# Layer 1's dilated convolution as row differences: four products for two output rows in place of six

## The chip, the cores and the metric

One Trainium2 chip, one core of it. The metric is the device time in microseconds (us) of one execution of the kernel.

## The reference

Two layers run one after the other on an input of 32 images, 128 channels, 56 x 56 pixels, all in fp32. Layer 0 is a depthwise 7 x 7 convolution, a layer norm, and a mixture of eight experts with two experts for each token and a capacity for each expert; its result is added to the input and to the normed convolution. Layer 1 takes that as `x`:

```python
feat = conv2d(x, conv_w, padding=DIL, dilation=DIL)      # 3x3, DIL = 3, 128 -> 64 channels
feat = batchnorm(feat, bn1_g, bn1_b, bn1_m, bn1_v)
feat = jax.nn.gelu(feat, approximate=False)
F2 = jnp.fft.fft2(feat.astype(jnp.float32), axes=(-2, -1))
...
out_f = jnp.abs(jnp.fft.ifft2(out_f, axes=(-2, -1)))     # attention over 8 channels of a head
...
gate = jnp.abs(jnp.fft.ifft2(gate, axes=(-2, -1)))       # F2 times a sigmoid gate
y = jnp.concatenate([out_f, gate], axis=1)
return y + x
```

The change concerns the first line: output row h is the sum over three kernel rows of products with the input rows h - 3, h and h + 3.

## The kernel before

**Layer 0.** The depthwise convolution and the norm write tokens to `xf` in HBM. The search for each expert's capacity and the lists of its tokens follow, and the experts run one after the other: tokens are gathered from `xf` (line 1048), multiplied by `W1` (line 1071, `ph`) and `W2` (line 1089, `py`), and stored to `yf` by slot. Expert 7 is the last.

**The gathers of layer 1.** A token of layer 1 is the sum of its row of `xf` and two rows of `yf`. A *row* here is a block of 8 image rows of two images, 7 x 128 tokens. `release` (line 458) issues one indirect DMA on GpSimd's queue (POOL) that gathers 128 tokens into a slice of a tile `y`; fourteen make a row, seven rows make a pair of images, and 16 pairs make 1568 gathers. `total` adds the two `y` tiles of a row to `xa` (line 474, two tensor_tensor on VectorE, each of 128 x 896) and stores the sum to `xsum`. `bring` makes sure of the sum and loads the row from `xsum` again; `place` turns it (line 1290) and adds it with beta to the padded input `xp` in SBUF (line 1294).

Each gather waits for the matmul that was the newest when the gather sixteen places ahead of it was asked for (`gated`, with `leash["n"]` of 16), and for one of six `y` tiles, which are three rows. How far apart gathers are asked for in the program is `PACE`, in units of matmul columns, of which MAIN counts those of `back` and FRONT those of `front`. `total` of a row comes in the program two rows ahead of its `place` at the latest, so VectorE, which works its queue in order, meets the wait for the last gather of a row at that point. The first gathers are issued while expert 7 still runs.

**Layer 1's two halves.** `front(pr)` makes the input of a pair of images and convolves it: for each block of 8 rows nine taps, each tap a matmul of 448 columns for either image (line 1305), the two images in the two halves of the array's columns (64 output channels each) and of the bank `pf`, then one Gelu with scale and shift on ScalarE (line 1313). `back(pr)` does the transforms as turns and products (lines 1348 and 1356), the Gram product `pg` (line 1380), the attention (lines 1445 and 1446), the gate (line 1494) and the outputs `oa` and `ob` (lines 1461 and 1524). VectorE copies each turned bank to `mid` (line 1335), ScalarE copies the products out (line 1359).

**The order.** It is written out by generators: while `back(pr)` runs, `front(pr + 1)` is fed in after the first sixth of MAIN, in proportion to the columns done. `front(0)` runs alone ahead of the loop and `back(15)` alone at its end. Each yield of `front` is the grain in which it is fed: 448 columns for a `place`, 1344 for three taps.

Pools that the change touches: `d4` (four `xp` tiles), `d6` (six `xa` and six `y`), `ring` (six `mid`, and six `o` that hold `oa` and `ob`), `psum_f` (two banks `pf`).

Of the kernel before, what the change touches and what calls it, by code (L numbers as in the profile page):

```python
# [38 lines left out]
C = 128  # L39
H = W = 56  # L40
RP = 59
# [33 lines left out]
def conv_seq_kernel(ctx: ExitStack, tc: tile.TileContext, t: dict, out: bass.AP, dbg: dict):  # L75
# [366 lines left out]
    def release():  # L442
# [6 lines left out]
        if k == 0:  # L449
            xs = d6.tile([128, NB, C], F32, name="xa", tag="xa")  # L450
            nc.sync.dma_start(out=xs, in_=xfv[:, r * NB : (r + 1) * NB, :])
            begun_[r] = xs, []
# [46 lines left out]
    def inputs(pr):  # L499
        xps = [d4.tile([C, XL], F32, name="xp") for i in range(2)]  # L500
        for i in range(2):
            nc.sync.dma_start(out=xps[i], in_=t["xp"][pr + i * HI])
        return xps
# [21 lines left out]
    if True:  # L525
# [638 lines left out]
        for e in range(E):  # L1164
# [6 lines left out]
            if e == E - 1:  # L1171
# [5 lines left out]
                d4 = ctx.enter_context(tc.tile_pool(name="d4", bufs=4))  # L1177
                d6 = ctx.enter_context(tc.tile_pool(name="d6", bufs=6))
# [62 lines left out]
    d2 = ctx.enter_context(tc.tile_pool(name="d2", bufs=2))  # L1241
    ring = ctx.enter_context(tc.tile_pool(name="ring", bufs=6))
    psum = ctx.enter_context(tc.tile_pool(name="psum_d", bufs=5, space=PSUM))
# [21 lines left out]
    bsc, bsh = batchnorm("bn1")  # L1265

# [16 lines left out]
    def place(r, xps):  # L1283
        xs, rb = rows.pop(r), r % NB
        for m0 in range(0, NB, 4):
# [5 lines left out]
            for i in range(2):  # L1291
                px = interior(xps[i], rb * P8, P8)[:, :, m0 * P8 : (m0 + nm) * P8]
# [4 lines left out]

    def front(pr, xps, feat):


        def taps(pf, g, k0):
            for k in range(k0, k0 + 3):
                o = ((k // 3) * 3 + 8 * g) * RP + (k % 3) * 3
                for i in range(2):
                    step["pe"] = nc.tensor.matmul(  # L1305
                        pf[i * DD : (i + 1) * DD, : 8 * W],
                        lhsT=cw[:, k, :],
                        rhs=xps[i][:, o : o + 8 * RP].rearrange("p (h w) -> p h w", w=RP)[:, :, :W],
                        start=(k == 0),
                        stop=(k == 8),  # L1310
                    )
            if k0 == 6:
                nc.scalar.activation(  # L1313
                    feat[:, 8 * g * W : 8 * (g + 1) * W], pf[:, : 8 * W], AF.Gelu, scale=bsc, bias=bsh
                )

# [5 lines left out]
        for g in range(NB):  # L1322
            if g + 1 < NB:
                place(pr * NB + g + 1, xps)
                bring(pr * NB + g + 3)
                yield NB * 64
            pf = psumf.tile([128, 512], F32, name="pf")
# [369 lines left out]
```

## Time and profile before

| | |
|---|---|
| median of three runs | 5202.68 us (5199.97 to 5206.07) |
| the profiled execution's own time | 4783.52 us |
| its span, first to last instruction | 4781.7 us |
| mean granted TensorE clock | 0.972 |
| busy: PE, DVE, ACT, POOL | 4479.7, 2812.1, 2087.5, 2627.5 us |
| first gather of layer 1's rows begins, last one ends | 2583.2 us, 4656.0 us |
| first matmul of layer 1's convolution | about 2795 us |

PE is TensorE, PEld its weight loads, DVE VectorE, ACT ScalarE, POOL GpSimd. An fp32 matmul or weight load stands in the trace as two records, one for each pass, so the 2016 matmuls of the convolution are 4032 records. Matmuls of the two images run beside each other. A group row names the line, the engine, the tiles written and read, the shape and the count; behind the first bar stand the busy time in us and the mean duration of one in ns, behind the second the idle time ahead of the group. In the timeline and the chain the first number is the start and the second the length, in us.

### The profile page before, as it was taken

What the parts mean: (1) busy time and instruction counts of PE and PEld (TensorE: products, weight loads), DVE (VectorE), ACT (ScalarE), POOL (GpSimd) and SP (SyncE); (2) the same over time, 40 slices, a digit from 0 to 9 for tenths busy, and PEclk for the clock granted to TensorE, in tenths of its full rate; (3) what the DMA queues carried; (4) which work ended last, traced back from release to release, by engine and by line L of the source; (5) the groups of instructions that cost most, each with busy time, mean ns of one, the idle gap of its engine ahead of it and who ended that gap; (6) DMA issues with size and microseconds to landing.
All of it is one profiled execution on the core that took longest, in us unless ns stands there. A gap on an engine that the chain in (4) does not pass through costs nothing.

```text
span 4781.7 us, 87262 instructions
## 1 busy us (share of the span) xinstructions
PE 4479.7 (94%) x33034; PEld 3134.7 (66%) x33034; DVE 2812.1 (59%) x5863; ACT 2087.5 (44%) x4260; POOL 2627.5 (55%) x2633
## 2 busy tenths in 40 slices
PE   7888872899999999999999989999999999999999
PEld 6777762577777777777777755666565555555556
DVE  4778787786857685735212325555555555555556
ACT  2657672344444444444444423333333333333334
POOL 0000010455555666666663777777677777777770
PEclk9999985899999999999999999999999999999999
DMA  9989953122222233333336766666666766666652
GB/s 251 268 253 268 271 157 99 49 63 65 67 69 70 77 84 84 87 87 89 86 89 191 187 150 179 181 182 183 177 174 183 184 185 175 178 184 178 184 154 59
DMA packets 767736, 705.23 MB, mean 147 GB/s; under 512 B 73231, under 2 KB 679568, under 8 KB 763220
## 3 DMA queue, kind: packets, MB, share of 16 engines
q1 hardware_dynamic: 597060, 487.55, 34.3%
q0 software_dynamic: 81664, 167.15, 16.2%
q10 hardware_dynamic: 88592, 44.96, 3.3%
q8 instruction: 261, 4.28, 0.4%
q14 instruction: 159, 1.30, 0.1%
HBM read 472.99 MB, written 226.39 MB: 146 GB/s over the span
## 4 chain that ended last, share of the span: by engine, by line
PE 75%; DVE 3%; DMA 3%; issue 2%; POOL 1%; ACT 0%; DVEq 0%; SPq 0%; POOLq 0%; ACTq 0%
PE py L1089 18%; PE ph L1071 17%; PE pf L1305 16%; PE pm L1356 8%; PE pt L1348 4%; PE pxt L1054 2%; PE pg L1380 2%; DMA y<-yf,slot 2%; PE pre L1445 2%; PE pxs L1290 2%; PE pim L1446 2%; DVE junk L716 1%; POOL y L458 1%; PE pid L956 1%; PE pn L745 1%
## 5 line engine op out<-in xcount | busy, mean ns | idle before, releaser
L458 POOL DMA_INDIRECT y<-yf,slot x1568 | 1567.0, 999 | 559.7 <-issue 318.6
L1048 POOL DMA_INDIRECT xg<-xf,ids x861 | 914.0, 1062 | 670.9 <-PE py L1089 294.2
L1089 PEld LDWEIGHTS py<-W,hT 128*128 128x128 f32 x7872 | 918.7, 191 | 101.2 <-issue 58.4
L1089 PE MATMUL py<-W,hT 128*128 128x128 f32 x7872 | 932.5, 276 | 0.0
L1071 PE MATMUL ph<-xT,W 128*128 128x512 f32 (+1 forms) x1984 | 895.3, 590 | 0.0
L1305 PE MATMUL pf<-xp,cw 128*64 128x448 f32 x4032 | 886.7, 549 | 0.1
L1074 ACT ACTIVATE hT<-ph,b1t 128x512 f32<-128x512 f32 (+1 forms) x992 | 620.5, 671 | 58.5 <-PE ph L1071 44.3
L1123 ACT ACTIVATE yo<-yo,gates 128x128 f32<-128x128 f32 x861 | 275.2, 390 | 840.2 <-DVE yo L1103 840.2
L1103 DVE TENSOR_TENSOR yo<-py,b2t 128x512 f32<-128x512 f32 (+2 forms) x256 | 170.5, 669 | 716.0 <-issue 527.3
L1071 PEld LDWEIGHTS ph<-xT,W 128*128 128x128 f32 x1984 | 354.9, 191 | 327.8 <-issue 317.0
L1305 PEld LDWEIGHTS pf<-xp,cw 128*64 128x64 f32 x4032 | 276.4, 135 | 410.7 <-issue 373.9
L1335 DVE COPY mid<-pt 112x512 f32<-112x512 f32 (+3 forms) x480 | 308.3, 661 | 292.1 <-PE pt L1348 287.9
L220 POOL TENSOR_SCALAR y<-y,sd,nb 128x128 f32<-128x128 f32 x49 | 24.6, 517 | 694.3 <-PE plq L277 693.1
L474 DVE TENSOR_TENSOR xa<-xa,y 128x896 f32<-128x896 f32 x224 | 243.7, 1088 | 111.4 <-DMA y<-yf,slot 101.2
L225 ACT ACTIVATE y<-y,nb,sd 128x128 f32<-128x128 f32 x735 | 287.7, 482 | 31.6 <-DVE nb L212 31.6
L1359 ACT COPY T<-pm 128x464 f32<-128x464 f32 (+2 forms) x240 | 124.2, 519 | 379.9 <-PE pm L1356 379.8
L174 PE MATMUL psa<-xt,stay 112*64 112x98 f32 (+1 forms) x4608 | 229.1, 258 | 42.7 <-DVE y L182 23.2
L174 PEld LDWEIGHTS psa<-xt,stay 112*64 112x64 f32 (+1 forms) x4608 | 214.7, 144 | 53.3 <-DVE y L182 31.1
L182 DVE TENSOR_TENSOR y<-psa,dwbB 128x392 f32<-128x392 f32 x256 | 140.4, 557 | 174.6 <-PE psa L174 131.5
L1294 DVE SCALAR_TENSOR_TENSOR xp<-pxs,beta,xp 128x256 f32<-128x256 f32 x448 | 172.3, 444 | 91.9 <-PE pxs L1290 82.0
L1313 ACT ACTIVATE feat<-pf,bn_shift,bn_scale 128x448 f32<-128x448 f32 x112 | 81.0, 724 | 306.9 <-PE pf L1305 306.4
L716 DVE TENSOR_SCALAR_CACHE_REDUCE junk<-key,trial 112x896 f32<-112x896 f32 x168 | 188.7, 1145 | 4.2
(412 smaller groups left out, 6028.7 us busy)
## 6 DMA issues: line engine op xcount, KB each, us to landing
xt<-in_x_dram SPq DMA_DIRECT2D x256, 392.0 KB
yf<-yo SPq DMA_DIRECT2D x240, 256.0 KB
xp<-in_xp_dram SPq DMA_DIRECT2D x32, 1832.0 KB
xa<-xf SPq DMA_DIRECT2D x112, 448.0 KB
xsum<-xa SPq DMA_DIRECT2D x112, 448.0 KB
xs<-xsum SPq DMA_DIRECT2D x112, 448.0 KB
xf<-y ACTq DMA_DIRECT2D x42, 1024.0 KB
y<-yf,slot POOLq DMA_INDIRECT x1568
```

Of the source, the lines that this page charges most:

```text
L174: nc.tensor.matmul(ps[h * 64 : (h + 1) * 64, c * TG : (c + 1) * TG], lhsT=wts[b][:, c4 + c, :], rhs=xv[: PKS[b], c, h, :, b * NB : b * NB ...
L225: nc.scalar.activation(yi, yi, AF.Identity, scale=sd[:, i : i + 1], bias=nb[:, i : i + 1])
L458: gated(marks[max(0, n - leash["n"])], nc.gpsimd.indirect_dma_start(out=begun_[r][1][-1][:, m, :], out_offset=None, in_=yf[: 1 + reach(r), :],
L474: nc.vector.tensor_tensor(out=xs, in0=xs, in1=y, op=ALU.add)
L1048: paced(2 * q, nc.gpsimd.indirect_dma_start(out=xg[:n, q, :], out_offset=None, in_=xf, in_offset=bass.IndirectOffsetOnAxis(ap=ids[:n, c0 + ...
L1071: step["pe"] = nc.tensor.matmul(ph[:, :ns], lhsT=W1[:, e, f * C : (f + 1) * C], rhs=xT[:, :ns], start=True, stop=True)
L1074: gelu = nc.scalar.activation(hT[:, f, :ns], ph[:, :ns], AF.Gelu, bias=b1t[:, e, f : f + 1])
L1089: step["pe"] = nc.tensor.matmul(py[:n, q * C : (q + 1) * C], lhsT=hT[:, f, q * 128 : q * 128 + n], rhs=W2[:, e, f, :], start=(f == 0), sto ...
L1123: nc.scalar.activation(yo[:n, q], yo[:n, q], AF.Copy, scale=gates[:n, c0 + q : c0 + q + 1])
L1305: step["pe"] = nc.tensor.matmul(pf[i * DD : (i + 1) * DD, : 8 * W], lhsT=cw[:, k, :], rhs=xps[i][:, o : o + 8 * RP].rearrange("p (h w) -> ...
L1335: step["dve"] = nc.vector.tensor_copy(to, of)
L1356: step["pe"] = nc.tensor.matmul(pm[:, i * M : (i + 1) * M], lhsT=mid[:m, i, :], rhs=by, start=True, stop=True)
```

## The change

For input rows d0, d3, d6 and d9 that lie three apart, and the three kernel rows g0, g1 and g2, the output rows h and h + 3 are

    m0 = (d0 - d6) g0        m1 = (d6 + d3) (g0 + g1 + g2)/2
    m2 = (d6 - d3) (g0 - g1 + g2)/2      m3 = (d9 - d3) g2
    row h = m0 + m1 + m2,    row h + 3 = m1 - m2 + m3

with three column taps in each product. A group is six output rows (three times two); there are nine full groups and one of two rows, which takes three products.

- Once, ahead of layer 1: four small VectorE operations make the mixed weights.
- `lift`: for each group four tensor_tensor on VectorE, SBUF to SBUF, both images at once, 128 x 2 x 180 elements (121 in the last group, three of them), into `tt` (five buffers), one group ahead of its products.
- `taps`: 24 matmuls of 168 columns for a full group (18 of 112 for the last) into two banks `pf`, `mid_` (m1, m2) and `side` (m0, m3).
- Out of PSUM: ScalarE copies `mid_` to `feat`; VectorE adds m1 to `side` in place, then makes the two row sets from `side` and `feat`; Gelu runs on `feat` in place.
- In two of the four transforms of `back` the copies to `mid` of every other bank go from VectorE to ScalarE (`shared=True`).
- The two images' `xp` become one tile (`dx`, two buffers); `xa` has four buffers in place of six; `oa` and `ob` get a pool of their own with five buffers; FRONT, and so PACE, follow the smaller count of columns. The order of the gathers on POOL's queue is as before.

```diff
@@ release
-            xs = d6.tile([128, NB, C], F32, name="xa", tag="xa")
+            xs = d4.tile([128, NB, C], F32, name="xa", tag="xa")
@@ inputs
-        xps = [d4.tile([C, XL], F32, name="xp") for i in range(2)]
+        xp = dx.tile([C, 2, XL], F32, name="xp")
...
@@ weights
+    mixed = d1.tile([C, 2, 3, DD], F32, name="mixed")
+    cu = [cw[:, 0:3, :], mixed[:, 0], mixed[:, 1], cw[:, 6:9, :]]
+    nc.vector.tensor_tensor(out=cu[2], in0=cu[0], in1=cu[3], op=ALU.add)
+    nc.vector.tensor_tensor(out=cu[1], in0=cu[2], in1=cw[:, 3:6, :], op=ALU.add)
+    nc.vector.tensor_tensor(out=cu[2], in0=cu[2], in1=cw[:, 3:6, :], op=ALU.subtract)
+    nc.vector.tensor_scalar(out=mixed, in0=mixed, scalar1=0.5, scalar2=None, op0=ALU.mult)
@@ front
+    SEED = {0: (0, 6, ALU.subtract), 1: (6, 3, ALU.add), 2: (6, 3, ALU.subtract), 3: (9, 3, ALU.subtract)}
+        def lift(g):
+            n, ms = lines(g)
+            k = n * RP + 3
+            tt = {}
+            for m in (1, 2, 0, 3)[: len(ms)]:
+                tt[m] = d5.tile([128, 2, SL], F32, name="tt")
+                a, b, op = SEED[m]
+                at = [(GR * g + r) * RP for r in (a, b)]
+                step["dve"] = nc.vector.tensor_tensor(
+                    out=tt[m][:, :, :k], in0=xps[:, :, at[0] : at[0] + k], in1=xps[:, :, at[1] : at[1] + k], op=op
+                )
+            return tt
+        def taps(g, tt):
...
+            for pair_ in ((1, 2), (0, 3)):
+                pf = psumf.tile([128, 512], F32, name="pf")
...
+                nc.scalar.copy(od, mid_)
+                nc.vector.tensor_tensor(
+                    out=side, in0=side, in1=od[:, 0:1].broadcast_to([128, 2, nw]), op=ALU.add
+                )
+                nc.vector.tensor_tensor(out=od[:, 0], in0=side[:, 0], in1=od[:, 1], op=ALU.add)
+                step["dve"] = nc.vector.tensor_tensor(out=od[:, 1], in0=side[:, 1], in1=od[:, 1], op=ALU.subtract)
+            nc.scalar.activation(od, od, AF.Gelu, scale=bsc, bias=bsh)
...
-        for g in range(NB):
-            if g + 1 < NB:
-                place(pr * NB + g + 1, xps)
-                bring(pr * NB + g + 3)
-                yield NB * 64
-            pf = psumf.tile([128, 512], F32, name="pf")
-            for k0 in (0, 3, 6):
-                taps(pf, g, k0)
-                yield 3 * 8 * W
+        placed, lifted = 1, []
+        for g in range(NGR):
+            while placed <= min(NB - 1, (GR * g + 8) // P8):
+                place(pr * NB + placed, xps)
+                bring(pr * NB + placed + 2)
+                placed += 1
+                yield NB * 64
+            lifted.append((g, lift(g)))
+            if len(lifted) == 2:
+                k = lifted.pop(0)
+                taps(*k)
+                yield load_of(k[0])
+        taps(*lifted[0])
+        yield load_of(NGR - 1)
@@ transform
-            dve(mid[:m, :ni, :].rearrange("p i c -> p (i c)"), pt[:m, : ni * 128])
+            (act if shared and i0 % 8 else dve)(mid[:m, :ni, :].rearrange("p i c -> p (i c)"), pt[:m, : ni * 128])
@@ outputs (oa and ob alike)
-                oa = ring.tile([128, 8 * W], F32, name="oa", tag="o")
+                oa = outs.tile([128, 8 * W], F32, name="oa", tag="o")
@@ pace
-    FRONT = NB * (NB * 64 + 9 * 8 * W)
+    FRONT = NB * NB * 64 + sum(load_of(g) for g in range(NGR))
```

## Prediction

> **What bounds the kernel now.** I read the page first (busy shares, groups), then the windows of layer 1, the chain of waits, and the timelines of GpSimd and VectorE.
>
> ```profile
> PE 4479.7 (94%) x33034; PEld 3134.7 (66%) x33034; DVE 2812.1 (59%) x5863; ACT 2087.5 (44%) x4260; POOL 2627.5 (55%) x2633
> L458 POOL DMA_INDIRECT y<-yf,slot x1568 | 1567.0, 999 | 559.7 <-issue 318.6
> L1305 PE MATMUL pf<-xp,cw 128*64 128x448 f32 x4032 | 886.7, 549 | 0.1
> ```
>
> PE is busy 94% and the convolution to be changed is 886.7 us of it by the page; POOL at 55% looks idle. That share is an average over stages. The windows of layer 1 alone (columns: stretch, length, then PE, PEld, DVE, ACT and POOL busy with their counts, clock, DMA share, GB/s):
>
> ```profile
> 3100.00:3300.00 200.00, 200.00 (x1251) 122.84 (x1249) 113.36 (x198) 77.65 (x128) 153.18 (x152) 1.00 0.67 178
> 3934.00:4650.00 716.00, 691.85 (x4195) 417.08 (x4196) 394.14 (x673) 249.09 (x413) 547.82 (x549) 0.99 0.67 179
> ```
>
> In the first, PE has no idle time. In the second it has 24 us, and POOL makes 549 gathers in 716 us, 1.304 us each. In the chain of waits the same piece of the convolution recurs once per pair of images:
>
> ```profile
> 3089.86 6.92 PE pf L1305 x36
> ...
> 3812.79 6.92 PE pf L1305 x36
> ...
> 3914.78 7.25 DMA y<-yf,slot
> ...
> 3934.42 6.92 PE pf L1305 x36
> ...
> 4701.02 6.92 PE pf L1305 x36
> ```
>
> From 3089.86 to 3812.79 are six pairs at 120.5 us; from 3934.42 to 4701.02 six at 127.8 us. A pair needs 98 gathers, and 98 x 1.304 = 127.8. So PE sets the pace only until about 3900; then the gathers do, and the chain shows waits for `y<-yf,slot`. Is POOL really full? Its timeline:
>
> ```profile
> 3322.74 0.94 POOL L458 DMA_INDIRECT y<-yf,slot  x1 [0.30 <-issue]
> 3323.99 1.47 POOL L458 DMA_INDIRECT y<-yf,slot  x1 [0.30 <-PE pt L1348]
> 3325.76 1.42 POOL L458 DMA_INDIRECT y<-yf,slot  x1 [0.30 <-issue]
> 3327.48 0.94 POOL L458 DMA_INDIRECT y<-yf,slot  x1 [0.30 <-issue]
> ```
>
> ```profile
> 3323.55 1.09 DVE L474 TENSOR_TENSOR xa<-xa,y 128x896 f32<-128x896 f32 x1
> 3324.67 0.69 DVE L1335 COPY mid<-pt 116x512 f32<-116x512 f32 x1
> 3325.28 1.08 DVE L474 TENSOR_TENSOR xa<-xa,y 128x896 f32<-128x896 f32 x1
> ```
>
> There is 0.30 us between gathers whatever the releaser's name: a fixed gap, not a wait. All gathers with that gap take 1567.0 + 1568 x 0.305 = 2045 us. They begin at 2583.2, so they can't end before 4628; they do end at 4656.0. POOL has 28 us of slack in 2073. The timelines show one thing more: both long gathers (1.47, 1.42) end 0.82 us after an `xa` addition ends (3324.64 and 3326.36). Of the 173 gathers over 1 us, 165 lie beside an L474 or the gate's L1494, and between two such operations in succession a gather gets in.
>
> **What the Trainium skill says.** "SBUF — State Buffer", section "Who interferes with whom", states that a VectorE instruction with two SBUF inputs contends with a GpSimd instruction that reads SBUF, and that the later one waits for the whole of the other. The trace agrees in its long gathers, though the page itself counts tensor_tensor as harmless to descriptor writing. "VectorE: DVE Perf Modes", "The perf-mode tier table", gives fp32 tensor_tensor one element per cycle; here 928 elements take 1129 ns and 580 take 753 (L1494), 1.08 ns per element and 127 ns fixed. "TensorE: Matmul & The Clock Gate", "LDWEIGHTS (loading the stationary operand)", has the load go by columns; the trace has 141 ns for 128 columns in `pxs`, and 0.14 us for the two of 64 of a tap.
>
> **The change part by part, in us per pair of images.**
>
> *PE.* 6.92 us are 18 slots of two images' matmuls, so a slot of 448 columns is 384 ns. Layer 0's depthwise convolution also has 64 output columns and two halves side by side: the timeline from 99.77 has 52 records of 98 columns in 2.40 us, 92 ns a slot. The line through both is 0.834 ns per column and 10.7 ns fixed: 151 ns at 168 columns, 104 ns at 112. A full group: 24 x 0.151 = 3.62; the last 18 x 0.104 = 1.87. New: 9 x 3.62 + 1.87 = 34.4; old: 7 x 6.92 = 48.4. PE saves 14.0 a pair, 224 in 16, and its pace becomes 106.5. A slot can't be under 140 (168 x 0.834); with its two weight loads in line behind the products it would be 151 + 140 = 291 and the change slower by itself. I take 151: layer 0's slots of 92 ns are shorter than two loads, so loads run beside products.
>
> *VectorE.* Added: 36 lifts of 360 elements at 127 + 389 = 516 ns and three of 242 at 388 (SBUF rate, from L1494): 19.7; nine `side` sums of 336 at about 500 ns and eighteen of 168 at 315 (from `ob`, 448 elements in 623 ns): 10.2; the last group's two, 0.5. Removed: six `mid` copies at 687 ns and one at 292: 4.4. Net +26. Now it is busy 113.36/200 x 120.5 = 68; it becomes 94 of about 128. Hidden under the gathers' pace, not under a pace of 106 with waits.
>
> *ScalarE.* Nine copies of 336 elements (about 0.43 each), seven `mid` copies (0.6 each, 3.7), Gelus in ten pieces (+0.9), up to three more table loads of 1.28: at most +13 on 47. Hidden.
>
> *POOL.* As many gathers in the same order. But each lift reads SBUF twice. Long gathers cost 1567.0 - 1568 x 0.944 = 87 us over 288 additions, 0.30 each; the loss goes with the square of the length (the chance to be hit times the wait). A lift of 360 against 896 elements: 0.30 x 0.16 = 0.05; 624 of them: 31 us in all. Below: 0, if lifts fall in gaps. Above: 138, if four in a row hold as one piece of 1.5 us (1.5²/(2 x 1.3) = 0.87, times 160 groups). I take 31, since gathers get in between additions in succession.
>
> *Queues and buffers.* SP has the same DMAs. `xa` with four buffers is no new wait while `y` allows three rows. PACE shrinks with the work, so a gather is asked for at the same share of a pair, and POOL's gate (a matmul sixteen gathers back) opens earlier. The four weight operations cost 2 us once, under the lead of gathers.
>
> **The sum.** PE's 14 us a pair come off a path that POOL holds at 98 x 1.304 = 127.8. What can be won is POOL's slack, 28 us. Last gather: 4656 - 28 + 31 = 4659. The tail from there was 4781.7 - 4656.0 = 126: the rest of `front(15)` and of `back(14)`, then `back(15)`. The last `total` comes after 37% of `front`'s columns where it came after 46%, so more of a shorter `front` is left: about 26 us for 30 of convolution and placing, 37 for 31 of `back(14)`: +2, and -2 for `mid` copies that two engines now share. End at 4659 + 126 = 4785 beside 4781.7; with 1.8 around the span 4787 against 4783.5. That is no change, within 10 us.
>
> The runs' median is 419 us above the profiled execution, and nothing in it says where those lie. If they lie where the change doesn't reach, 5203 stays 5203.
>
> **The rivals.**
>
> *A, the forecast: gathers hold the pace.* 5203, own range 5175 to 5235. For: 98 x 1.304 is the period. Chance 0.36, of it 0.11 below by over 0.2%, 0.13 within, 0.12 above.
>
> *B: in the runs PE is the slow part.* If the 419 us are PE's, it is slower by 419/4480 = 9.4%, a pair takes 131.8 and the gathers are covered throughout. Then the change runs into them: start 2583 x 1.094 = 2825, + 2045 + 31 = 4901, + 138 = 5039, or 5041 (-3.1%). Against: the profile has clock 1.00 in layer 1. Chance 0.30.
>
> *C: VectorE's queue takes over, slower.* While a gather is late, VectorE stands at L474 and lifts, sums and copies queue behind it; lifts also wait for `tt` buffers until the products ahead have read them. In the 18.4 us of a row it has 13.4 of work; once waits exceed 5 us, the row gets longer, and with it the release of `y`. At 0.6 us over, 0.6 x 112 = 67: 5270. The upper bound of the lifts' hold on POOL ends there too and beyond. For: L474 waited 101.2 us for gathers already. Chance 0.28.
>
> *D: the saving arrives whole,* gathers off the path in the runs: 5203 - 224 = 4979. Chance 0.06. That the products don't get cheaper (slots near 210 ns, where 9.5 groups cost the old 48 us) ends with A, since PE then stays at its 120.
>
> **How the numbers follow.** A difference of 0.2% is about what a measurement of this kernel can tell. Faster: B + D + 0.11 = 0.47; within: 0.13; slower: 0.28 + 0.12 = 0.40. The range runs from a little below B, 5005, to above C, 5290; D and the tails of B and C are left out.
>
> **What would show it.** Right: gathers still 1.30 us apart from about 3300 on, last one near 4659, PE with 15 to 20 us idle a pair, a full group of products in 3.6 us, VectorE's lifts near 0.52 us, PE's chain full of `y<-yf,slot`. C: gathers with gaps over 0.31 us while VectorE is busy above 85%. B can't be seen in the profile: there A holds and the runs alone gain. Wrong if the gathers come closer than 1.245 us, or if slots stay near 0.2 us.

## The result, and the profile after

| | before | changed |
|---|---|---|
| median of four runs each | 5204.38 us (5199.97 to 5216.09) | 5401.62 us (5399.95 to 5405.66) |
| ratio, 95% interval | | 1.0381 (1.0359 to 1.0402) |
| profiled execution, its span | 4783.52, 4781.7 us | 5400.09, 5398.2 us |
| mean granted TensorE clock | 0.972 | 0.915 |

The change makes the kernel 3.8% slower. The two profiles can't be laid side by side as they are: the profiled execution of before took 4784 us, while the runs, and the profile of the changed kernel beside them, are from a chip that gives the kernel before 5204. I call them a 4780 chip and a 5200 chip; the experiments found four chips of the first kind and two of the second, and both kernels were profiled on both. No chip came up in two rounds of experiments, so the names say what a chip gave then and not that it always does.

First the profile on the 5200 chip, the lines that answer to those of before. The busy line, the gathers and the products of the convolution:

```profile
PE 4539.3 (84%) x36490; PEld 3538.7 (66%) x36490; DVE 3165.3 (59%) x6843; ACT 2269.4 (42%) x4625; POOL 2677.3 (50%) x2633
L458 POOL DMA_INDIRECT y<-yf,slot x1568 | 1614.8, 1030 | 1085.4 <-issue 360.6
L1350 PE MATMUL pf<-tt,cw 128*64 128x168 f32 (+1 forms) x3648 | 400.4, 342 | 251.1 <-issue 116.2
L1350 PE MATMUL pf<-tt,mixed 128*64 128x168 f32 (+1 forms) x3840 | 385.2, 328 | 49.7 <-issue 25.7
```

The busy time of L1350 is not to be compared with the 886.7 us of L1305, since a shorter matmul's record holds more of its latency. What matters is behind the second bar: the products wait 300 us, where L1305 waited 0.1, and the idle time ahead of gathers is 1085 us where it was 560. The windows of layer 1 (stretch, length, PE, PEld, DVE, ACT, POOL, clock, DMA share, GB/s):

```profile
3100.00:3300.00 200.00, 166.44 (x1400) 134.60 (x1397) 126.76 (x257) 73.56 (x129) 124.17 (x120) 0.95 0.60 163
3934.00:4650.00 716.00, 536.22 (x4099) 417.19 (x4098) 402.61 (x788) 244.20 (x414) 440.63 (x421) 0.86 0.53 139
```

In the second, 421 gathers stand where 549 stood, 1.70 us each. POOL is busy 62%, VectorE 56%, TensorE 75%: no engine is full. The chain of waits from 4300 to 4400 says what they wait for:

```profile
by line: another core or an unknown queue 33.1%; PE pm L1418 18.6%; PE pf L1350 14.7%; PE pg L1442 7.2%; PE pt L1410 6.9%; issue 6.7%; ACT T L1421 2.8%; DVE xp L1303 1.9%; ACT root L1518 1.5%; ACT L1372 1.3%; ACT L1518 1.3%; ACT mid L1412 1
...
4326.55 9.55 another core or an unknown queue
...
4345.25 9.00 another core or an unknown queue
```

and the timeline shows one such piece:

```profile
4326.15 2.05 PE L1418 MATMUL pm<-ih,mid 116*128 116x112 f32 x8 [4.92 <-issue]
...
4327.99 1.06 PE L1410 MATMUL pt<-ident,Z 128*116 128x128 f32 x4
...
4332.25 0.94 POOL L458 DMA_INDIRECT y<-yf,slot  x1 [0.31 <-issue]
4336.12 0.53 ACT L1421 COPY T<-pm 128x448 f32<-128x448 f32 x1 [9.57 <-remote]
4336.18 0.69 DVE L1397 COPY mid<-pt 116x512 f32<-116x512 f32 x1 [8.98 <-remote]
4336.42 0.94 POOL L458 DMA_INDIRECT y<-yf,slot  x1 [3.23 <-remote]
```

TensorE's products and turns are done at 4328.2 and 4329.1. ScalarE and VectorE, which wait for just these, go on at 4336.1, both at once, and POOL, whose gate is a matmul too, with them. There is one core, so "remote" names nothing that the profile knows. For seven us all engines but POOL stand, and POOL issues one gather.

### The profile page after: what moved, and what is told of

It reads as the page before. It is cut to its first block, busy times and chain, and to the rows that moved or that the text cites. A ratio compares the mean times of both kernels' runs of the same rounds, so it can differ in the third digit from the quotient of the medians.

```text
span 5398.2 us, 95683 instructions
## 1 busy us (share of the span) xinstructions
PE 4539.3 (84%) x36490; PEld 3538.7 (66%) x36490; DVE 3165.3 (59%) x6843; ACT 2269.4 (42%) x4625; POOL 2677.3 (50%) x2633
## 4 chain that ended last, share of the span: by engine, by line
PE 65%; issue 6%; another core or an unknown queue 6%; DVE 5%; ACT 3%; POOL 0%; DMA 0%; DVEq 0%; SPq 0%; ACTq 0%; POOLq 0%
PE py L1089 16%; PE ph L1071 15%; PE pf L1350 12%; PE pm L1418 8%; PE pt L1410 3%; PE pxt L1054 2%; PE pg L1442 2%; PE pre L1507 2%; PE pim L1508 2%; PE pxs L1299 2%; DVE xp L1303 1%; DVE junk L716 1%; PE pid L956 1%; PE pn L745 1%
## 5 line engine op out<-in xcount | busy, mean ns | idle before, releaser
L458 POOL DMA_INDIRECT y<-yf,slot x1568 | 1614.8, 1030 | 1085.4 <-issue 360.6
L1089 PEld LDWEIGHTS py<-W,hT 128*128 128x128 f32 x7872 | 927.2, 192 | 135.1 <-issue 115.1
L1089 PE MATMUL py<-W,hT 128*128 128x128 f32 x7872 | 946.7, 277 | 29.3 <-issue 28.9
L1071 PE MATMUL ph<-xT,W 128*128 128x512 f32 (+1 forms) x1984 | 906.9, 597 | 0.6 <-issue 0.5
L1350 PE MATMUL pf<-tt,cw 128*64 128x168 f32 (+1 forms) x3648 | 400.4, 342 | 251.1 <-issue 116.2
L1350 PEld LDWEIGHTS pf<-tt,cw 128*64 128x64 f32 x3648 | 300.4, 153 | 319.5 <-issue 175.2
L1350 PE MATMUL pf<-tt,mixed 128*64 128x168 f32 (+1 forms) x3840 | 385.2, 328 | 49.7 <-issue 25.7
L1397 DVE COPY mid<-pt 112x512 f32<-112x512 f32 (+2 forms) x368 | 245.2, 669 | 265.7 <-PE pt L1410 99.8
L1333 DVE TENSOR_TENSOR tt<-xp 128x360 f32<-128x360 f32 (+1 forms) x624 | 299.0, 519 | 140.5 <-remote 48.2
L1350 PEld LDWEIGHTS pf<-tt,mixed 128*64 128x64 f32 x3840 | 282.6, 146 | 148.6 <-issue 94.0
L1366 ACT COPY feat<-pf 128x336 f32<-128x336 f32 x144 | 63.2, 439 | 570.5 <-remote 289.0
L1421 ACT COPY T<-pm 128x464 f32<-128x464 f32 (+2 forms) x240 | 122.4, 521 | 332.0 <-PE pm L1418 170.2
```

What stands on the lines that cost most here:

```text
L458: gated(marks[max(0, n - leash["n"])], nc.gpsimd.indirect_dma_start(out=begun_[r][1][-1][:, m, :], out_offset=None, in_=yf[: 1 + reach(r), :],
L1071: step["pe"] = nc.tensor.matmul(ph[:, :ns], lhsT=W1[:, e, f * C : (f + 1) * C], rhs=xT[:, :ns], start=True, stop=True)
L1089: step["pe"] = nc.tensor.matmul(py[:n, q * C : (q + 1) * C], lhsT=hT[:, f, q * 128 : q * 128 + n], rhs=W2[:, e, f, :], start=(f == 0), sto ...
L1333: step["dve"] = nc.vector.tensor_tensor(out=tt[m][:, :, :k], in0=xps[:, :, at[0] : at[0] + k], in1=xps[:, :, at[1] : at[1] + k], op=op)
L1350: step["pe"] = nc.tensor.matmul(pf[i * DD : (i + 1) * DD, j * 3 * W : j * 3 * W + nw], lhsT=cu[m][:, k, :], rhs=tt[m][:, i, 3 * k : 3 * k ...
L1397: step["dve"] = nc.vector.tensor_copy(to, of)
```

## The experiments

Durations of stages were read from the traces: a pair's period from one pair's first `pg` to the next, the gathers' *loss* as what their durations exceed 0.944 us by, the gathers' *pauses* as what gaps of over 0.35 us exceed 0.305 by. All runs up to `e14_after_halves` were on 4780 chips. A time without a range is a single run; the kernel before spreads over 4775 to 4795 us on these chips.

### Without the gathers, and without the lifts

`e1_before`: the kernel before unchanged.

> The kernel before, unchanged. The profiled execution of before took 4784 us, its runs 5204, the runs of the changed kernel 5402. If the missing 420 us are stalls of TensorE like those in the trace of the changed kernel (engines that stand together for 5 to 10 us though the matmuls they wait for had been started), this profile ends near 5200 with PE idle near 10% in layer 1 and matmuls late even in the experts' stage. If those stalls belong to the change alone, the profile is like the one before: about 4780, PE without idle time until 3900.

Measured: 4776.97 us; loss 78.3 us, last gather's end 4651.

`e2_before_plain` and `e3_after_plain`: in either kernel the gathers of layer 1 become plain DMAs of as many bytes on SP's queue; they read other rows of `yf` than the reference wants.

```diff
-        gated(marks[max(0, n - leash["n"])], nc.gpsimd.indirect_dma_start(
-            out=begun_[r][1][-1][:, m, :],
...
+        if m == 0:
+            at = 1 + (2 * r + k // NB) * 128 % 8192
+            nc.sync.dma_start(
+                out=begun_[r][1][-1], in_=yf[at : at + NB * 128, :].rearrange("(q p) c -> p q c", p=128)
+            )
```

> The kernel before with layer 1's 1568 gathers left out: each tile of seven slices is filled by one plain DMA of as many rows of yf at fixed places, from SP's queue, with no gate (the sums are of wrong tokens). If gathers set the pace of before, layer 1 falls to the pace of TensorE, 120 us a pair or less, and the time is 100 to 400 us under that of before. If TensorE stalls by itself, the time stays within 50 us of 5200.

> The same in the changed kernel: no gathers in layer 1. If gathers and what holds them up (lifts on the port, late y tiles) are the bound, a pair falls from 152 us to about 107 and the time to about 4750, under e2_before_plain by up to 220 us. If the bound is VectorE's and ScalarE's queue around the products (rival C), or TensorE's stalls, it stays above 5200.

Measured: 4743.81 and 4636.75 us, beside 4776.97 and 4783.61 of the unchanged kernel before. Both expectations counted from 5200 us; on this chip the kernel before gains 33 to 40 us by losing its gathers. Without gathers the change gains 107 us, 2.3%. The window 3300 to 3700 of the kernel before and of the changed one, in this order:

```profile
3300.00:3700.00 400.00, 399.99 (x2465) 241.73 (x2465) 233.62 (x399) 142.22 (x236) 0.00 (x0) 1.00 0.63 183
```

```profile
3300.00:3700.00 400.00, 370.11 (x3234) 304.29 (x3234) 308.86 (x619) 190.32 (x327) 0.00 (x0) 0.97 0.67 191
```

TensorE is full before and has 30 us of 400 idle after. A pair takes 115.3 us on average, and 0.925 of that is 106.7 of work: the prediction's 106.5. TensorE's busy time in the whole run falls by 4470.1 - 4257.4 = 213 us (224 were worked out). Half of that is given back as waits, the longest groups of which are for lifts (29.1 us in 3000 to 4400) and for `mid` on VectorE (15.8).

`e4_after_nolift`: the changed kernel without lifts; the products read `xp` itself, so the convolution is another one.

```diff
-                tt[m] = d5.tile([128, 2, SL], F32, name="tt")
                 a, b, op = SEED[m]
...
+                at = (GR * g + b) * RP
+                tt[m] = xps[:, :, at : min(at + SL, XL)]
```

> The changed kernel with the lifts left out: the products read xp itself at one of the two row sets (so the convolution is of wrong rows), all else as it is. If the 624 lifts on VectorE (20 us a pair, and their reads against the gathers) make it slow, it gains 150 us or more on the changed kernel's 5402. If it is the small matmuls, the two banks or the stalls, under 50 us.

Measured: 4758.25 us, 25 us under before and 85 under the changed kernel on such a chip (`e5_after`, below). The first four pairs take 112 to 116 us, from the sixth on 127.4 to 130.7, the last excepted. Gathers stand 0.305 us apart throughout (pauses 0.9 us in all), loss 95.5 us. So POOL's slack, 28 us by the prediction, is about all that a faster TensorE won here while the gathers were there. This kernel has `xa` with four buffers too, and hardly a pause, so the fewer buffers bring none.

### The lifts and the gathers

`e5_after`: the changed kernel, unchanged, on a 4780 chip.

> The changed kernel, unchanged, beside the kernel before, which in the last experiments took 4777 to 4784 us and not 5204. If the gathers bound both (128 us a pair), it ends within 20 us of before, near 4785: the 3.8% of the result then come from what the runs of the result had and these don't. If the change itself brings waits on TensorE (152 us a pair in its profile), it stays 3 to 4% behind, near 4960 or more.

Measured: 4843.69 us (4832.01 to 4851.14) beside 4783.85; ratio 1.0127 (1.0106 to 1.0148). That lies between the two expectations. The gathers' row of the page, the window 3300 to 3700, and a piece of the timeline:

```profile
L458 POOL DMA_INDIRECT y<-yf,slot x1568 | 1643.5, 1048 | 532.9 <-issue 328.4
```

```profile
3300.00:3700.00 400.00, 342.63 (x2907) 284.42 (x2905) 279.37 (x552) 169.70 (x294) 310.53 (x294) 0.91 0.65 174
```

```profile
2832.38 1.85 DVE L1333 TENSOR_TENSOR tt<-xp 128x360 f32<-128x360 f32 x4
2832.50 2.55 POOL L458 DMA_INDIRECT y<-yf,slot  x1 [0.30 <-issue]
...
2834.15 0.50 DVE L1367 TENSOR_TENSOR pf<-pf,feat 128x336 f32<-128x336 f32 x1
```

The loss is 1643.5 - 1568 x 0.944 = 163.3 us where it was 84.5 (`e10_before`, below), and 294 gathers in 400 us are 1.36 each: 98 x 1.36 = 133, the period from the sixth pair on. The timeline shows how. Four lifts run one behind the other from 2832.38 to 2834.23; the gather that began 0.12 us into the first ends at 2835.05, 0.82 us after the *last* of them. It did not get in between. Counted over the trace, for gathers that lost over 0.1 us: 206 were held by one operation and lost 90 us (159 in the kernel before lost 81); 40 were held by two to seven in a row and lost 66. It is not so every time: where a lift that held a gather was followed directly by another, 28 gathers were held on and 17 got in between.

`e6_before_lifts`: the kernel before with 39 additions of two SBUF operands of 360 elements per pair, which nothing reads, and `xa` with four buffers as in the changed kernel.

```diff
+            for m in range(6 if g < 4 else 5):
+                tt = d5.tile([128, 368], F32, name="tt")
+                a = (8 * g + m % 3) * RP
+                step["dve"] = nc.vector.tensor_tensor(
+                    out=tt[:, :360], in0=xps[0][:, a : a + 360], in1=xps[1][:, a : a + 360], op=ALU.add
+                )
             pf = psumf.tile([128, 512], F32, name="pf")
```

> The kernel before with 39 additions of 360 elements a pair on VectorE, SBUF to SBUF, whose results nobody reads, and xa with four buffers. If a lift costs the gathers 0.05 us as estimated (31 us in all), it ends within 40 us of 4780, with long gathers of 110 to 120 us in sum where before has 78 to 87. If four lifts in a row hold a gather for 1.5 us, 100 us or more above. If VectorE's queue is the bound, gaps open between gathers.

Measured: 4857.41 us, loss 170.5 us; again between the expectations. The additions, with the old convolution, cost 74 us, and leaving the lifts out of the changed kernel saved 85: the cost is that of the lifts, not of what else the change does. One gather was held for 7.67 us, by a run of eleven additions and gate multiplications.

`e7_after_dvemid`: the changed kernel with all `mid` copies on VectorE again.

```diff
-            (act if shared and i0 % 8 else dve)(mid[:m, :ni, :].rearrange("p i c -> p (i c)"), pt[:m, : ni * 128])
+            dve(mid[:m, :ni, :].rearrange("p i c -> p (i c)"), pt[:m, : ni * 128])
```

> The changed kernel with the mid copies of all four transforms on VectorE again (+4.4 us of VectorE a pair, 3.7 less on ScalarE). If VectorE's queue is at its limit, a pair takes 2 to 5 us longer than in the changed kernel, 30 to 80 us in all; if gathers are the bound, no difference within 10 us.

Measured: 4844.89 us, loss 164.4 us: no difference from `e5_after`. Where `mid` is copied shows no effect.

`e8_after_gap`: a fill ahead of each lift, in order.

```diff
+                with tc.issue_after(step["dve"].ins):
+                    nc.vector.memset(tt[m][:, 0, :], 0.0)
                 a, b, op = SEED[m]
```

> The changed kernel with one more VectorE operation ahead of each lift: a fill of half of the lift's own tile (184 elements, no operand read from SBUF), put in order so that fill and lift alternate and no two lifts stand next to each other. It adds 624 operations to VectorE and removes nothing. Theory H (a run of lifts that stand one behind the other holds a gather for the whole run): the gathers' loss beside lifts, 84 us in the changed kernel, falls to 31 to 55 although VectorE has more to do; spacing of gathers from about 3300 on falls from 1.36 to about 1.33 us; 4790 to 4825 where the changed kernel has 4844. Theory Q (VectorE's queue is too full, and what comes behind the lifts in it is late): 624 more operations make it worse, 4850 to 4900. Theory P (each lift holds a gather by itself at 0.13 us, wherever it stands): 84 us stay, 4840 to 4855.

Measured: 4810.36 us (4804.47 to 4812.38), ratio to before 1.0057 (1.0041 to 1.0074). Loss beside lifts 36.7 us (84.0 in `e5_after`), and no gather was held by more than one lift. The timeline:

```profile
3507.30 0.21 DVE L1332 MEMSET tt<- 128x184 f32 x1
3507.41 0.94 POOL L458 DMA_INDIRECT y<-yf,slot  x1 [0.30 <-issue]
...
3507.62 0.52 DVE L1335 TENSOR_TENSOR tt<-xp 128x360 f32<-128x360 f32 x1
```

VectorE has 624 operations more to do, and the kernel is 33 us faster. So these 33 us were not VectorE's queue but runs of lifts. The 36.7 us that stay are near the 31 of the prediction, which priced lifts one by one.

`e9_after_spread`: the lifts of a group set apart in the program, one each ahead of, between and behind the products and sums of the group before, each kept behind the latest copy.

```diff
-            lifted.append((g, lift(g)))
+            tt = {}
+            lift(g, tt, (1,) if lifted else (1, 2, 0, 3))
+            lifted.append((g, tt))
...
+                if tt2 is not None and pair_[0]:
+                    lift(g2, tt2, (2,))
+                    yield load_of(g) // 2
```

> The changed kernel with the four lifts of a group set apart: one ahead of the products of the group before, one between that group's two sets of products, one ahead of and one behind its sums, and each kept behind the last VectorE work in the program, so that copies and sums with a PSUM operand come between most of them. The work is the same, nothing is added. H: loss of gathers beside lifts 40 to 60 us in place of 84, 4800 to 4830. Q: no change from 4844, or slower by the new waits of VectorE for products, 4850 and more. P: 84 us and 4840 to 4850.

Measured: 4835.21 us (4833.01 to 4836.87), loss beside lifts 94.3 us. A miss, and its trace says why: 44% of the lifts still follow the one before within 0.6 us (56% in `e5_after`), and some runs got longer, up to eight with `xa` additions among them; nine such runs lost 41 us. Spreading in the program is not spreading on the engine.

`e11_before_reduce`: as `e6_before_lifts`, in the same order on VectorE, but each operation a sum along one operand.

```diff
-                step["dve"] = nc.vector.tensor_tensor(
-                    out=tt[:, :360], in0=xps[0][:, a : a + 360], in1=xps[1][:, a : a + 360], op=ALU.add
-                )
+                step["dve"] = nc.vector.tensor_reduce(
+                    out=tt[:, :1], in_=xps[m % 2][:, a : a + 360], op=ALU.add, axis=AX.X
+                )
```

> The kernel before with 39 operations per pair that nothing reads, in the same places and in the same order as the 39 unread additions that made it 4857 us, but each is a sum over 360 elements along one operand from SBUF, with one element written. VectorE's time is about the same. Theory H (two operands from SBUF hold the gathers): the loss of gathers goes back to 80 to 100 us as in the kernel before, 4780 to 4800. Theory Q (the time that VectorE spends, in whatever operation): as with additions, 4845 to 4870.

`e10_before`, unchanged, ran beside it.

> The kernel before unchanged, for its trace on this chip. If this chip gives it about 4780, it shows the gathers 1.304 us apart again and ends near 4780. If it gives it about 5200 as in the runs of the result, the trace shows where the 420 us lie: theory T (TensorE's counts reach the other engines late, as seen in the changed kernel's trace) wants stretches in which several engines resume together while TensorE's matmuls were done before, from about 1600 on and most of them after 2600; theory G (gathers or other DMAs slower) wants gathers more than 1.31 us apart with POOL full.

Measured: 4824.5 us beside 4782.41. The sums take 518 ns each, as long as a lift. The loss is 105.5 us, against 170.5 with additions and 84.5 in `e10_before`. In the timeline three sums pass a gather by, and four gate multiplications in a row hold the next:

```profile
3777.87 1.39 DVE L1331 TENSOR_REDUCE tt<-xp 128x1 f32<-128x360 f32 x3
3778.20 0.94 POOL L458 DMA_INDIRECT y<-yf,slot  x1 [0.30 <-issue]
3779.17 3.86 DVE L1501 TENSOR_TENSOR Z<-Z,gt 128x928 f32<-128x928 f32 x4
3779.45 4.40 POOL L458 DMA_INDIRECT y<-yf,slot  x1 [0.30 <-issue]
```

"SBUF — State Buffer", section "Who interferes with whom", says just this of one operand and of two; the runs agree, 0.94 against 4.40 us. No gather was held by a sum. But the time is 25 us above what I expected: 20 of the loss are such runs of the gate, and pauses are 53.4 us where they were 28.9. Additions cost 74 us, sums of the same length 42: VectorE's time costs something by itself, and the second operand costs the rest (each a single run, on two chips).

### Can the saving be had?

`e12_after_split` (changed) and `e13_before_split` (before): a fill of 64 elements ahead of each lift, `xa` addition and gate multiplication, and each `xa` addition cut in two. `e14_after_halves`: as the first, with each lift cut in two as well.

```diff
+    def fill():
+        with tc.issue_after(step["dve"].ins):
+            step["dve"] = nc.vector.memset(pad, 0.0)
...
-            for y in ys:
-                nc.vector.tensor_tensor(out=xs, in0=xs, in1=y, op=ALU.add)
+        for y in ys:
+            for p in (slice(0, 4), slice(4, NB)):
+                fill()
+                with tc.issue_after(step["dve"].ins):
+                    step["dve"] = nc.vector.tensor_tensor(
+                        out=xs[:, p, :], in0=xs[:, p, :], in1=y[:, p, :], op=ALU.add
+                    )
```

> The changed kernel with a fill of 64 elements (no operand read) kept ahead of each lift, of each xa addition and of each gate multiplication, and each xa addition cut in two (512 and 384 elements). Same results, 16 fills and 2 additions more per row and pair than needed by the sums. Theory H (an operation with two operands from SBUF holds a gather until it ends, and so does an unbroken run of them; the loss of a set-apart one goes with the square of its length): lifts lose 37 as with the longer fill, xa about 32 in place of 60, the gate 10 in place of 18: 75 to 85 in all in place of 163; last gather near 4640, 4765 to 4780, so a little below the kernel before (4783). If a fill as short as this is not enough for a gather to get in, runs hold on, and it is 4830 to 4850. Theory Q (VectorE's queue): 4845 to 4880.

> The kernel before with the same fills and cut additions (it has no lifts). H: loss of gathers about 45 in place of 84; the gathers' pace becomes 98 x (1.250 + 0.03), about 125 us, near TensorE's own 120.5; the end is then 4745 to 4765. This tells how much of what the run above gains has to do with the change at all. If both land within 10 us of each other, the change is worth nothing as long as gathers set the pace, in either direction.

> As the changed kernel with fills and cut additions, and each lift cut in two as well (one image each, 180 elements, a fill ahead of each). H: lifts lose about half of 37, the whole 57 to 70, last gather near 4620: 4745 to 4765. Theory Q: VectorE gets some 78 operations more per pair, and 117 of 127 us to do; if its queue decides, gathers show gaps of more than 0.31 us and the time goes up, 4790 to 4850.

| | median | ratio to before | loss | pauses |
|---|---|---|---|---|
| `e12_after_split` | 4792.10 | 1.0026 (1.0019 to 1.0032) | 93.7 | 19.3 |
| `e13_before_split` | 4768.56 | 0.9972 (0.9962 to 0.9983) | 69.2 | 33.6 |
| `e14_after_halves` | 4835.79 | 1.0112 (1.0095 to 1.0129) | 87.5 | 55.0 |

A fill of 0.11 us is mostly enough, but not always: of the gathers that lost over 0.1 us beside an operation with a fill behind it, 161 got in behind that operation and 8 were held on through the fill in the first kernel, 108 and 4 in the second, 171 and 17 in the third. (Behind the 0.21 us fills of `e8_after_gap` it was 23 and none.) One gather of `e13_before_split`, held through four parts of `xa` additions and the three fills between them:

```profile
3067.21 0.62 DVE L483 TENSOR_TENSOR xa<-xa,y 128x512 f32<-128x512 f32 x1
3067.34 2.90 POOL L458 DMA_INDIRECT y<-yf,slot  x1 [0.30 <-issue]
3067.80 0.11 DVE L470 MEMSET pad<- 128x64 f32 x1
...
3068.94 0.49 DVE L483 TENSOR_TENSOR xa<-xa,y 128x384 f32<-128x384 f32 x1
```

The first kernel is 12 us above its range, its loss 9 above. Its gathers end where those of the kernel before do (4654.7 and 4655.3); what it lacks is in the time from there to the end, 139.4 us against 125.3. The second is 4 us above its range, its loss 69 where 45 was expected. The third is a miss: its lifts lose 29 us, hardly less than 31, the pauses grow, and from the last gather to the end it takes 149.1 us. It has more VectorE operations than the first; that these are the cause isn't shown apart. The best kernel of all with its gathers is the *old* convolution with fills: 0.28% under before. The changed convolution does not get under before in any form tried that keeps its lifts and its gathers; the gathers' own 98 x 1.249 = 122.4 us a pair already exceed TensorE's old 120.5.

### The 5200 chips

`e15_before` and `e16_after`, both unchanged, on one chip; `e17_after_split_plain` and `e18_before_plain` on another: `e12_after_split` and the kernel before, with plain DMAs in place of the gathers of layer 1, as in `e2_before_plain`.

> The kernel before unchanged. If this chip gives about 4780: gathers 1.30 us apart in the second half of layer 1, as on the chips before. If it gives about 5200 as in the runs of the result: theory T (counts of TensorE's matmuls reach the other engines late) wants hold-ups of several engines at once which end together, from about 1600 on; theory G wants gathers longer than 1.0 us on average or gaps above 0.31 us that no wait explains.

> The changed kernel unchanged, on the same chip as the one beside it. At about 4780 for the kernel before: 4830 to 4850, with about 40 gathers held by runs of two to seven additions, 60 to 70 us lost in them. At about 5200: theory T, 5400, with pairs of 140 to 170 us and hold-ups as in the result's trace; then the difference of the two traces by stage shows how much of the 200 us is gathers held by lifts and how much is hold-ups.

> The changed kernel with fills ahead of its two-operand additions and cut xa additions, and with the gathers of layer 1 replaced by plain DMAs of the same bytes on SP's queue (it sums other rows of yf than the reference, and POOL does nothing in layer 1). If this chip gives the kernel before about 4780: with no gather to hold, the fills can only cost, so 4640 to 4660 beside the 4637 of the changed kernel with plain DMAs; 4690 and more would mean that VectorE's queue bounds it. If it gives about 5170: theory T1 (TensorE's late counts come with the gathers' descriptors or their DMAs) wants 4640 to 4700 and no bunches of counts; T2 (they belong to the chip and come without gathers too) wants 4900 to 5150 and bunches from about 1600 on as before.

> The kernel before with the gathers of layer 1 replaced by plain DMAs of the same bytes on SP's queue (other rows of yf than the reference's). On a chip that gives the kernel before about 4780: 4740 to 4746 as on the first one. On one that gives about 5170: T1 4745 to 4800 and no late counts after 2600; T2 4950 to 5150 and bunches of counts as in the kernel before there.

Measured: 5167.39 and 5352.28 us, a ratio of 1.036 (one run each). Then 4730.98 and 4767.09, on a chip that took 5219.33 for the kernel before. The stages, from the traces:

| us | before, 4780 (`e10_before`) | changed, 4780 (`e5_after`) | before, 5200 (`e15_before`) | changed, 5200 (`e16_after`) |
|---|---|---|---|---|
| first gather begins | 2584.3 | 2580.7 | 2599.1 | 2595.1 |
| gathers at 0.944 with gaps of 0.305 | 1958.1 | 1958.1 | 1958.1 | 1958.1 |
| loss | 84.5 | 163.3 | 72.0 | 135.1 |
| pauses | 28.9 | 1.4 | 396.8 | 521.1 |
| from the last gather to the end | 125.3 | 127.0 | 139.6 | 141.5 |
| span | 4780.6 | 4830.2 | 5165.6 | 5350.5 |

The gathers themselves are not slower on the 5200 chip; there are pauses between them, 368 us more of the 385 by which the kernel before is longer. One pause of `e15_before` in the timeline:

```profile
3980.50 6.99 PE L1305 MATMUL pf<-xp,cw 128*64 128x448 f32 x36
...
3987.42 1.52 PE L1348 MATMUL pt<-ident,Z 128*116 128x128 f32 x12
...
3999.10 0.72 ACT L1313 ACTIVATE feat<-pf,bn_shift,bn_scale 128x448 f32<-128x448 f32 x1 [18.73 <-remote]
3999.16 1.88 DVE L1335 COPY mid<-pt 116x512 f32<-116x512 f32 x3 [14.70 <-remote]
3999.33 0.94 POOL L458 DMA_INDIRECT y<-yf,slot  x1 [2.69 <-remote]
```

A *count* is the semaphore that TensorE raises at the end of a matmul and that other engines wait for. The convolution's last matmul of that group and three banks of turns each raise the one that ScalarE, VectorE and POOL wait for. The matmuls stand between 3986.9 and 3989.0; the four counts are recorded at 3999.07, 3999.13, 3999.19 and 3999.25, 10 to 12 us after them, all together.

The ends of matmuls are modelled in a profile, and here TensorE stands too, so by this piece alone the matmuls themselves might have been late. Another piece of the same trace speaks against that:

```profile
2914.56 3.93 PE L1305 MATMUL pf<-xp,cw 128*64 128x448 f32 x20
...
2918.42 0.98 PE L1290 MATMUL pxs<-ident,xs 128*128 128x128 f32 x7
...
2919.34 3.74 PE L1305 MATMUL pf<-xp,cw 128*64 128x448 f32 x17
...
2924.68 0.72 ACT L1313 ACTIVATE feat<-pf,bn_shift,bn_scale 128x448 f32<-128x448 f32 x1 [12.21 <-remote]
```

The Gelu at 2924.68 waits for nothing but the group whose last product ends at 2918.49, and starts 6.19 us after it, while TensorE goes on with 29 more matmul records. Over all 112 Gelus of the kernel before: in `e10_before` each starts within 0.1 us of its last product or of the ScalarE work before it, in `e15_before` 41 start over 0.5 us late, 144 us in sum, and in `e18_before_plain`, without layer 1's gathers, none does. The changed kernel's copy of `mid_` is never over 0.5 us late in `e5_after`, and 89 times of 144 in `e16_after`, 274 us in sum. So matmuls were done and their counts reached the engines late.

The counts' own records agree. Over 0.15 us from the end of any matmul that raises one lie, from 2580 on, 838 of 1766 recorded counts in `e15_before` and 1 of 1928 in `e18_before_plain`; ahead of POOL's first gather (at 848) none in either. (Where gathers run on the 5200 chips, many records of counts are missing.) The window 3300 to 3700 of `e18_before_plain`:

```profile
3300.00:3700.00 400.00, 399.99 (x2465) 242.29 (x2461) 234.45 (x401) 147.58 (x246) 0.00 (x0) 1.00 0.62 179
```

This is the window of `e2_before_plain` on the 4780 chip again. Without layer 1's gathers a 5200 chip is a 4780 chip there, and the 23 us that remain lie ahead of the first convolution (2824.8 against 2801.6), where the experts' gathers still run. So the late counts come with the gathers on POOL; which property of the gathers brings them isn't shown. Leaving out those of layer 1 saves 452 of 5219 us on this chip, where it saved 33 to 40 on a 4780 chip. `e17_after_split_plain` was expected at 4640 to 4700 in this case and took 4731: a pair takes 120.8 us on average where `e3_after_plain`, without fills, had 115.3, and the 25 us ahead of the first convolution come on top.

## Why the prediction was wrong

**PE step: right.** A full group of products, without a wait in it, takes 3.64 us in `e5_after` (from 3224.84 to 3228.48; 3.62 worked out), a pair 106.7 of TensorE (106.5), and the run 213 us less without gathers (224). One reading ahead of it says less than it seems to: the two weight loads of 64 columns of a tap start 5 ns apart and take 134 ns each, one of 128 columns takes 141 in `pxs` and 192 at `W2`. So this trace doesn't show a load's time going by its columns. The sum doesn't rest on it.

**DVE and ACT steps: right.** In `e5_after` lifts take 527 ns (516), `side` sums 511 (500), row sums 324 (315). In the window of `e5_after` VectorE works 279.37/400 x 133 = 93 us a pair (94), ScalarE 56 where it had 43 (+13 at most).

**Queues and buffers: right.** Four `xa` tiles bring no wait of their own: L474 waits for `y`, as before (189.8 us in `e5_after`, 101.4 in `e10_before`), and `e4_after_nolift` has the four tiles and no pauses.

**POOL step: the term that failed on 4780 chips.** "I take 31, since gathers get in between additions in succession." The loss rose by 79 us, lifts having 84 of it. The price of a lift by itself was about right (36.7 us in all where fills set them apart), and what I had seen in the trace of before was so: of the gathers there that lost over 0.1 us beside an `xa` addition or a gate multiplication with another directly behind it, 53 of 53 got in between, as here (two additions, 2619.26 to 2621.47, the first ending at 2620.35; the gather ends 0.81 us after that):

```profile
2619.26 2.21 DVE L474 TENSOR_TENSOR xa<-xa,y 128x896 f32<-128x896 f32 x2
```

```profile
2619.40 1.76 POOL L458 DMA_INDIRECT y<-yf,slot  x1 [0.30 <-PE ph L1071]
```

What failed was to carry that over to lifts: between two lifts 17 got in and 28 did not. The upper bound, "if four in a row hold as one piece", named the mechanism, but not its size: four lifts in a row are 1.85 us in the trace and 2.06 by the prediction's own 516 ns, not 1.5, which would put the bound at 210 to 260 in place of 138. Lifts lost 84. Why a gather gets in at one place and not at another isn't shown. Two `xa` additions stand 0.03 us apart in the trace and lifts overlap by 0.08, but gate multiplications overlap as well, and they let 27 of 27 in between in `e5_after` and 7 of 17 in `e11_before_reduce`.

**Sum: right in form.** The last gather was put at 4656 - 28 + 31 = 4659. It ended at 4703.2: the pauses did fall from 28.9 to 1.4, and 79 stood for 31. The tail was put at 126 and measured 127.0. With 79 the sum would have given +51 us; the profiled executions of `e5_after` and `e10_before` are 50 apart. (That of `e5_after` is the fastest of its four; the medians are 60 apart.)

**"If they lie where the change doesn't reach, 5203 stays 5203": wrong, and the larger error.** On a 5200 chip 368 of the 385 us lie in the pauses between the gathers of layer 1, in the midst of what is changed. From before to changed there the last gather moves by 183 us: 63 of loss and 124 of pauses, less 4 at the start. So about a third of the slowdown in these two traces is gathers held, and two thirds are pauses that the prediction put at nothing.

**Rivals.** B (TensorE is the slow part in the runs) fell: of the 385 us TensorE is busy in 128 (4608 against 4481 us) and idle in the rest, and without gathers its pairs take 121.4 us on either kind of chip. C named the right direction and not the reason. Its clause on the lifts' upper bound is what happened on 4780 chips; its main clause, VectorE over 85% busy with pauses behind `xa`, is not: VectorE is at 70% there and pauses are gone. D needed the gathers off the path; they stayed on it.

**Open.** Why gathers make TensorE's counts late on some chips and not on others, and why the changed kernel pays 124 us more for them. Of the pauses, 198 us in `e15_before` and 140 in `e16_after` end over 0.35 us after the last matmul that raises a count, which points to a late count. Most of the others end right behind such a matmul: 195 us before, 355 changed. So what grew are pauses in which TensorE seems to have been behind itself. One reading is that each group of the changed kernel passes from TensorE through ScalarE and VectorE and back, so that a late count finds less work in hand: in the trace of after the copies at L1366 wait 289 us for "remote". That is argued, not shown.

## What to carry to other kernels

Before you trade TensorE time for VectorE time, look at what VectorE's new operations do to a queue that is nearly full: here POOL had 28 us of slack, so 224 us of TensorE could win 28, and the lifts, with two SBUF operands each, took 79. Price such operations one by one for the low end and a run of them as one piece for the high end; what is seen beside one kind of them need not hold for another. A fill between them set most gathers free, at the price of VectorE's time; whether it does is read from the engine's order in the trace and not from the program's. When the runs and the profile of a kernel differ by 400 us, the forecast needs the profile of an execution that took as long as the runs; an assumption that the difference lies elsewhere is a coin toss.

## What the hardware showed that I had not expected

- VectorE operations with two SBUF operands that follow one another directly can hold a gather until the last of them ends: 3.97 us for one gather beside seven lifts, 4.40 beside four gate multiplications, 7.67 beside eleven operations in `e6_before_lifts`. They don't always: 53 of 53 gathers got in between them in the kernel before, 17 of 45 between two lifts in `e5_after`. A fill of 0.21 us between lifts ended it in all 23 cases of `e8_after_gap`, one of 0.11 us in 440 of 469.
- On two of the six chips of the experiments, TensorE's counts reached the waiting engines up to 12 us after its matmuls while gathers were being issued on POOL, and the kernel before took 385 to 440 us longer; without the gathers of layer 1 it took 23 us longer.
- The granted clock of TensorE was lower where it stood idle: in 3300 to 3700 it was 1.00 in the kernel before with no idle time, 0.97 in `e3_after_plain` with 30 us idle, and 0.91 in `e5_after` with 57 us idle. Which of the two brings the other, and what it costs, was not tested.
